# One flat list of steps for eight sequences, in another order

## The chip, the cores and the metric

The kernel runs on one NeuronCore of a Trainium2 chip. The number that counts is the time of one execution on the device in microseconds (us); of several executions the median is given. A profile is one execution recorded by the hardware: each instruction with its engine, its start and its length. The engines are TensorE (PE, matmuls; PEld is its weight load), VectorE (DVE), ScalarE (ACT), GpSimd (POOL) and SyncE (SP, which here issues nearly all DMAs). Each engine works through its own instructions in the order in which the program lists them, and waits where an operand or a buffer isn't ready.

## What is computed

Eight sequences of 512 tokens with 256 channels go through a feed-forward half step, causal attention with 16 heads, and the same feed-forward half step again; each has a layer norm ahead of it and a residual around it. A `butterfly` is ten stages of 2x2 mixing over 1024 channels. All is float32.

```python
x = x + 0.5 * ffn(layernorm(x))
x = x + attn(layernorm(x))
x = x + 0.5 * ffn(layernorm(x))

def ffn(x):      # the same weights both times
    h = butterfly(x @ W_exp + b_exp, up_weights)
    h = butterfly(gelu(h + up_bias), down_weights)
    return h @ W_con + b_con + down_bias

def attn(x):     # q, k, v: 16 heads of 32 channels
    scores = where(causal, q @ k.T / sqrt(16), -inf)
    return concat(softmax(scores) @ v) @ Wo
```

## The kernel before

**Folding.** At the start the butterflies are multiplied into the weights, so that a feed-forward is two products: up (256 to 1024, then gelu) and down (1024 to 256). While this is done, the up steps of sequence 0 and the first layer norm of sequence 1 are computed as well (lines 718 to 742). None of that is touched by the change.

**Steps.** After it, the whole work of all eight sequences is cut into steps of one to three microseconds of TensorE, and a list written out by hand in the source (`ORDER`, line 636) says in which order the steps are put into the program. Every engine's own order follows from this one list. A word of it is a letter, a number and a sequence; the letters are

- `f`, `g`: one of 8 up steps of the first and of the second feed-forward (`up_steps`, line 378): a product into a PSUM tile `ph`, then a gelu on ACT into the tile `g` (line 392). The first step of such a group allocates `g`; there is one buffer for it.
- `F`, `G`: one of 8 down half steps (`down_steps`, line 396): four of them fill one PSUM tile `py`, then DVE adds it to the residual `x` (line 414). `G` also stores `x` to DRAM (line 416).
- `s`, `a`, `x` with `1`, `a` or `2` for the three layer norms: statistics (DVE, with a power on POOL), normalization with a 32x32 transpose on DVE, and the way into the transposed tile `xnt`. Each comes in two halves. For nearly all, `x` is a pair of DMA steps: first a write to DRAM (`td`, line 365), then four reads back (`xnt`, line 372). For the attention norm of sequence 0 and the last norm of sequence 7 it is two transposes on TensorE (line 207) instead.
- `q`, `v`: one of 8 query and key steps, one of 4 value steps: a product into PSUM, then a copy by ACT (lines 437, 451).
- `u0` to `u9`: a unit of scores. TensorE writes `sc` (line 492), which is one tile of four PSUM banks for all units. DVE adds the causal mask and takes the row's minimum of the negated scores (line 506), then ACT takes the exponential (line 519). The ten units of a sequence are the entries of `UNITS`, line 465.
- `t`: DVE transposes a unit's exponentials into `pr` (line 537). `m`: DVE adds the transposed reciprocals of the row sums (line 547), then SP issues 16 DMAs that carry `pr` to the tile `pt` (line 563; one buffer). `p`: 32 matmul records of `pt` with `v` into `pa` (line 576), then a DVE product into `ot` (line 583). There are four groups of heads, so `m0` to `m3` and `p0` to `p3` for each sequence.
- `w`: one of 4 output products (`po`); two fill a PSUM tile, which DVE adds to `x` (line 602).
- `l`: the load of a later sequence's `x` (line 106).

The PSUM tiles of `f`, `g`, `F`, `G`, `q`, `v` and `w` share three buffers (`ps_a`). Exponential and gelu use different tables of ACT; a change from the one to the other shows as an `ACT_TABLE_LOAD` in the profile.

`ORDER` has one list for each sequence, and the loop at line 748 goes through them one after the other. A word's sequence is given relative to the list in which it stands: in the list of sequence 7, `w-1` is an output step of sequence 6, and `p-3` the last product of sequence 6. The lists of sequence 0 and 7 begin

```python
0: """7F+0 x1+1 sa+0 aa+0 F+0 sa+0 x1+1 2f+1 aa+0 xa+0 f+1 xa+0 f+1 s1+2 2q+0 f+1 s1+2 u0 a1+2 2q+0 u1 v
7: """q+0 u0 q+0 u1 2G-2 t0 u2 p-3 t1a w-1 t1b t2a G-2 m0 u3 w-1 G-2 s2-1 u4 v t2b v t4a t3 2w-1 t4b v
      s2-1 v p0 m1 q+0 2a2-1 q+0 u5 q+0 u6 t5 G-2 q+0 t6b u7 2x2-1 t6a G-2 t7a p1 m2 u8 2G-2 g-1 t8 2g-1
      u9 t9a 2g-1 l+1 g-1 t9b t7b p2 2g-1 2G-1 m3 3G-1 p3 2w+0 s2+0 2w+0 a2+0 s2+0 2G-1 a2+0 G-1 2x2+0 8g+0
```

Of the kernel before, what the change touches and what calls it, by code (L numbers as in the profile page):

```python
# [48 lines left out]
def macaron_kernel(  # L49
# [19 lines left out]
    B, N, C = x.shape  # L69
# [34 lines left out]
    def load_x(b):  # L104
        xt[b] = resid.tile([P, NT, C], F32, name=f"x_{b}", tag="x", bufs=4)
        nc.sync.dma_start(out=xt[b], in_=x[b].rearrange("(t p) c -> p t c", p=P))
# [358 lines left out]
    UNITS = [(0, 0), (1, 0), (2, 0), (0, 1), (1, 1), (0, 2), (1, 2), (2, 2), (0, 3), (1, 3)]  # L465
# [77 lines left out]
    def turn_sums(b, g):  # L543

        zr = lnp.tile([P, 4, NT], F32, name=f"zr_{b}_{g}", tag="zr")
        nc.vector.reciprocal(zr.rearrange("p h q -> p q h"), kept["zs", b][:, g])
        nc.vector.transpose(
            kept["pr", b, g][:, :, 4 * NSLOT :, :],
            zr.rearrange("p h (q o) -> p h q o", o=1).to_broadcast([P, 4, NT, 32]),
        )  # L550

    def move(b, g, pool):

        pr = kept.pop(("pr", b, g))
        pt = kept["pt", b, g] = pool.tile([P, 4, ROW, 32], F32, name=f"pt_{b}_{g}", tag="pt")
        ends = (b, g) == (B - 1, NG - 1)
        if ends:
            for i in range(4):
                nc.vector.tensor_copy(pt[bass.ts(i, 32), i], pr[bass.ts(i, 32), i])
        for d in range(1 if ends else 0, 4):  # L560
            for i in (0, 2, 1, 3):
                j = i ^ d
                nc.sync.dma_start(out=pt[bass.ts(j, 32), i], in_=pr[bass.ts(i, 32), j])  # L563
# [50 lines left out]
            else:  # L614
                step()

    def attention_steps(b, pool):
        def moved(g):
            turn_sums(b, g)
            move(b, g, pool)  # L620

        return {
            "u": lambda n: score_unit(b, *UNITS[n], pool),
            "t": lambda n, part=0: turn(b, *UNITS[n], part, pool),
            "m": moved,
            "p": lambda g: times_v(b, g, pool),
        }

    ORDER = {
        0: """7F+0 x1+1 sa+0 aa+0 F+0 sa+0 x1+1 2f+1 aa+0 xa+0 f+1 xa+0 f+1 s1+2 2q+0 f+1 s1+2 u0 a1+2 2q+0 u1 v
              q+0 v t0 t1b u2 v 2f+1 t1a f+1 t2a m0 a1+2 u3 t2b 2F+1 u4 x1+2 t3 2F+1 t4b sa+1 v x1+2 q+0 t4a F+1
              u5 p0 m1 t5 u6 3F+1 aa+1 sa+1 2q+0 u7 f+2 t6b aa+1 t6a f+2 xa+1 f+2 xa+1 u8 t7a p1 2f+2 m2 2f+2 t8
              f+2 q+1 t7b q+1 u9 q+1 t9a t9b 2q+1 p2 m3""",  # L640
        1: """u0 F+1 q+0 u1 2F+1 t0 u2 F+1 t1b 2q+0 t1a u3 t2a p-3 m0 u4 2w-1 s2-1 a2-1 w-1 v w-1 s2-1 v t2b a2-1
              F+1 u5 v t3 x2-1 sa+1 3F+1 t4b v x2-1 aa+1 u6 p0 2g-1 sa+1 s1+2 aa+1 t4a xa+1 m1 g-1 a1+2 t5 g-1
              s1+2 4g-1 G-1 u7 xa+1 G-1 a1+2 x1+2 t7a x1+2 4G-1 t6a t6b u8 p1 m2 u9 t8 2G-1 f+2 q+1 f+2 t7b t9b
              f+2 q+1 f+2 t9a f+2 q+1 p2 f+2 m3""",
        2: """u0 2q+0 u1 t0 q+0 2f+1 u2 2q+0 t1a u3 p-3 t2a t1b u4 m0 2w-1 F+1 t2b u5 F+1 t3 F+1 t4a w-1 t4b F+1
              l+2 s2-1 w-1 2v s2-1 v 2a2-1 v F+1 sa+1 x2-1 F+1 u6 p0 F+1 t6a x2-1 m1 F+1 t6b t5 aa+1 sa+1 aa+1
              xa+1 7g-1 u7 s1+2 g-1 G-1 u8 t7a p1 t7b xa+1 m2 a1+2 u9 2G-1 q+1 G-1 s1+2 a1+2 t8 t9b 3G-1 x1+2 G-1
              t9a q+1 x1+2 2q+1 p2 m3""",
        3: """u0 2q+0 l+2 f+1 t0 4f+1 u1 2f+1 u2 p-3 w-1 t1b w-1 s2-1 q+0 t2a t1a u3 t2b m0 v 2w-1 v u4 t3 q+0
              a2-1 v f+1 u5 s2-1 a2-1 t4b v t4a 4F+1 u6 p0 x2-1 F+1 x2-1 m1 sa+1 2F+1 s1+2 u7 F+1 sa+1 aa+1 4g-1  # L650
              t7a aa+1 t5 t6a 2g-1 t6b xa+1 u8 p1 g-1 xa+1 g-1 m2 t7b u9 q+1 s1+2 q+1 a1+2 G-1 t9a a1+2 x1+2 t8
              t9b 2G-1 q+1 x1+2 G-1 q+1 p2 m3""",
        4: """u0 3G-2 t0 q+0 u1 G-2 q+0 u2 t1b 2f+1 q+0 t1a u3 p-3 l+2 u4 w-1 t3 v w-1 f+1 t2a w-1 s2-1 m0 v w-1
              t4b s2-1 2f+1 t2b 2a2-1 q+0 f+1 v x2-1 f+1 2s1+2 f+1 2F+1 v u5 p0 u6 x2-1 F+1 t4a F+1 m1 F+1 u7 t6a
              3F+1 g-1 sa+1 t5 2g-1 aa+1 sa+1 aa+1 g-1 t7a 2g-1 t6b u8 p1 2xa+1 g-1 m2 a1+2 g-1 t8 G-1 u9 2G-1
              a1+2 q+1 t7b G-1 2x1+2 t9a 2q+1 G-1 q+1 t9b p2 m3""",
        5: """u0 3G-2 u1 q+0 t0 2q+0 u2 f+1 t1b 2f+1 t1a u3 p-3 u4 w-1 t2a v t2b w-1 s2-1 q+0 l+2 m0 f+1 s1+2 v t3
              v t4a f+1 u5 t4b a2-1 w-1 f+1 w-1 f+1 s2-1 a2-1 v x2-1 f+1 s1+2 F+1 u6 p0 x2-1 m1 t6b 2F+1 a1+2 u7
              3F+1 t5 a1+2 F+1 sa+1 F+1 g-1 t7a x1+2 sa+1 g-1 aa+1 2g-1 aa+1 u8 t6a xa+1 p1 xa+1 4g-1 m2 x1+2 u9
              t9b t8 2q+1 2G-1 q+1 G-1 t9a t7b G-1 p2 m3""",  # L660
        6: """u0 q+0 2G-2 u1 G-2 q+0 u2 G-2 t1a t1b 2f+1 t0 t2a 2f+1 u3 p-3 m0 u4 w-1 t2b w-1 v 2w-1 v s2-1 q+0 v
              t4b t4a v t3 s2-1 f+1 u5 p0 m1 2f+1 a2-1 t5 f+1 u6 q+0 a2-1 F+1 t6b q+0 F+1 u7 F+1 t6a F+1 x2-1 t7a
              p1 x2-1 t7b m2 u8 sa+1 3F+1 u9 F+1 2g-1 sa+1 aa+1 g-1 aa+1 g-1 xa+1 t9a g-1 t8 g-1 t9b p2 xa+1 2g-1
              2q+1 m3""",
        7: """q+0 u0 q+0 u1 2G-2 t0 u2 p-3 t1a w-1 t1b t2a G-2 m0 u3 w-1 G-2 s2-1 u4 v t2b v t4a t3 2w-1 t4b v
              s2-1 v p0 m1 q+0 2a2-1 q+0 u5 q+0 u6 t5 G-2 q+0 t6b u7 2x2-1 t6a G-2 t7a p1 m2 u8 2G-2 g-1 t8 2g-1
              u9 t9a 2g-1 l+1 g-1 t9b t7b p2 2g-1 2G-1 m3 3G-1 p3 2w+0 s2+0 2w+0 a2+0 s2+0 2G-1 a2+0 G-1 2x2+0 8g+0
              8G+0""",
    }
    LNS = {"a": "at", "1": "f1", "2": "f2"}  # L670
    queues = {}

    def next_of(key, b, make):
        if (key, b) not in queues:
            queues[key, b] = make()
        return queues[key, b].pop(0)

    def sequence(b, pool):
        for token in ORDER[b].split():
            times, rest = (int(token[0]), token[1:]) if token[0].isdigit() else (1, token)  # L680
            what, kind, at = rest[0], "", 0
            if what in "sax":
                kind, rest = rest[1], rest[1:]
            if what in "ut":
                part = "ab".find(rest[-1])
                n = int(rest[1]) if part >= 0 else int(rest[1:])
            elif len(rest) > 1:
                at = int(rest[1:])
            for _ in range(times):
                if what == "u":  # L690
                    attention_steps(b, pool)["u"](n)
                elif what == "t":
                    attention_steps(b, pool)["t"](n, max(part, 0))
                elif what == "m":
                    attention_steps(b, pool)["m"](at)
                elif what == "p":
                    attention_steps(b - (at < 0), pool)["p"](abs(at))
                elif what == "l":
                    if b + at < B:
                        load_x(b + at)  # L700
                elif b + at < B:
                    c, ln = b + at, LNS.get(kind)
                    make = {
                        "q": lambda: qk_steps(c),
                        "v": lambda: v_steps(c),
                        "w": lambda: wo_steps(c),
                        "f": lambda: up_steps(c, "f1"),
                        "F": lambda: down_steps(c, "f1", store=False),
                        "g": lambda: up_steps(c, "f2"),
                        "G": lambda: down_steps(c, "f2", store=True),  # L710
                        "s": lambda: [partial(ln_stats, c, ln, half) for half in range(2)],
                        "a": lambda: [partial(ln_apply, c, ln, half) for half in range(2)],
                        "x": lambda: ln_steps(c, ln),
                    }[what]
                    next_of(what + kind, c, make)()


    with fold, tc.manual_schedule():
        nc.scalar.activation(ones[:, :1], ones[:, 1:2], AF.Copy)
# [15 lines left out]
        for i in range(HIGH - 1, -1, -1):  # L735
            cur, _ = high_stage(cur, i, dnc_sb, "dn", C, NBLK // 2)
# [8 lines left out]
    ps_o = ctx.enter_context(tc.tile_pool(name="ps_o", bufs=1, space=bass.MemoryType.PSUM))  # L745
    with tc.tile_pool(name="attn", bufs=1) as attn, tc.manual_schedule():
        kept["sc"] = ps_u.tile([P, 4, 512], F32, name="sc", tag="u")
        for b in range(B):
            sequence(b, attn)


def _turned(x):
# [87 lines left out]
```

## Time and profile before

| | us |
|---|---|
| median of 3 runs | 872.11 (870.77 to 872.52) |
| the profiled execution, whole | 870.19 |
| its span, first to last instruction | 868.2 |
| TensorE busy | 847.7 |
| VectorE busy | 629.4 |
| ScalarE busy | 517.8 |
| GpSimd busy | 92.2 |
| DMA rows on SP's queue | 55.8% of 16 engines |

A row of the timeline reads: start in us from the span's start, length in us, engine, line, operation, the tiles written and read, shape, number of instructions, and in brackets how long the engine had been idle and what released it. A row of the waits reads: engine, tile and line that waited, what it waited for, then the total in us, the number of times and the longest. Ends of matmuls are modelled, so a step's length on TensorE is better read from one start to the next. fp32 matmuls appear as two records each: an `f`, `g`, `q` or `v` step is 16 records, an `F`, `G` or `w` step and a `p` step 32.

### The profile page before, as it was taken

The page shows a single profiled execution, that of the slowest core. Times are in us where ns is not written, and L with a number is a line of the kernel's source. Part 1 is how long each engine was busy: PE and PEld are TensorE (multiplying, and loading weights), DVE is VectorE, ACT ScalarE, POOL GpSimd, SP SyncE. Part 2 cuts the span into 40 slices and gives each one's busy share as a digit, 9 for nine tenths or more (in the row PEclk, how much of TensorE's full clock was granted, in tenths as well). Part 3 has the DMA queues.
Part 4 walks back from the last instruction along what each step waited for, and adds up shares of the span by engine and source line. Part 5 has one row for each costly group of instructions (what it writes and reads, how often), then busy time and mean ns, then how long its engine had stood idle before and what let it go on. Part 6 is the DMA issues. An engine that isn't in the chain of part 4 may idle for free.

```text
span 868.2 us, 28463 instructions
## 1 busy us (share of the span) xinstructions
PE 847.7 (98%) x11914; PEld 370.1 (43%) x11914; DVE 629.4 (73%) x1815; ACT 517.8 (60%) x1359; POOL 92.2 (11%) x123
## 2 busy tenths in 40 slices
PE   8999999999999999999999999999999999989898
PEld 7443524444334443443443434335344343433454
DVE  7948985997579685699777585888567794977430
ACT  6618686654585474776585654865746764747210
POOL 6511000011001010010102010021000100010010
PEclk9999999999999999999999999999999999999999
DMA  9210766637656568267765277557684577367400
GB/s 334 70 50 18 206 183 153 159 110 204 179 135 159 146 175 225 54 178 189 195 172 135 83 192 193 134 140 202 166 188 123 127 190 200 99 174 198 129 14 26
DMA packets 52832, 130.41 MB, mean 150 GB/s; under 512 B 10849, under 2 KB 32609, under 8 KB 52705
## 3 DMA queue, kind: packets, MB, share of 16 engines
q1 hardware_dynamic: 52560, 128.57, 55.8%
q8 instruction: 94, 1.54, 0.8%
q14 instruction: 34, 0.27, 0.1%
q10 hardware_dynamic: 144, 0.02, 0.0%
HBM read 21.80 MB, written 15.20 MB: 43 GB/s over the span
## 4 chain that ended last, share of the span: by engine, by line
PE 80%; SPq 5%; DVE 5%; DMA 4%; ACT 3%; issue 1%; DVEq 0%; ACTq 0%
PE ph_f L352 22%; PE py_f L352 22%; PE pp L352 11%; PE sc L492 8%; PE po L352 6%; PE pv L352 6%; SPq L563 5%; PE pa L576 5%; DVE e L506 3%; DMA out_dram<-x 1%; ACT e L519 1%; DMA pt<-pr 1%; DVE pr L537 1%; DMA wexp_sb<-in_wexp_t_dram 1%; DMA x<-in_x_dram 1%
## 5 line engine op out<-in xcount | busy, mean ns | idle before, releaser
L519 ACT ACTIVATE e<-e,nm 128x128 f32<-128x128 f32 (+3 forms) x512 | 280.4, 549 | 93.6 <-DVE nm L506 93.2
L506 DVE CUSTOM_DVE_ANT_0 e<-sc,mask 128x384 f32<-128x384 f32 (+2 forms) x384 | 196.4, 552 | 98.4 <-PE sc L492 97.8
L352 PE MATMUL py_f<-wdn_sb,g_f 128*32 128x256 f32 x4096 | 232.4, 380 | 0.0
L352 PE MATMUL ph_f<-xnt_f,wup_sb 128*32 128x512 f32 x2048 | 228.6, 593 | 0.6 <-ACT g_f L392 0.3
L537 DVE STREAM_TRANSPOSE pr<-e 128x1536 f32<-128x1536 f32 (+2 forms) x128 | 171.2, 1356 | 19.8 <-ACT e L519 19.8
L352 PEld LDWEIGHTS py_f<-wdn_sb,g_f 128*32 128x32 f32 x4096 | 131.9, 110 | 100.2 <-issue 19.3
L392 ACT ACTIVATE g_f<-ph_f,bup_sb 128x512 f32<-128x512 f32 x128 | 84.7, 686 | 90.6 <-PE ph_f L352 90.1
L352 PEld LDWEIGHTS ph_f<-xnt_f,wup_sb 128*32 128x32 f32 x2048 | 65.2, 110 | 139.7 <-issue 113.7
L519 ACT ACTIVATION_READ_ACCUMULATOR e<-e,nm 128x1 f32 x512 | 96.0, 188 | 0.0
L492 PE MATMUL sc<-kt,qt 32*64 32x512 f32 (+5 forms) x2048 | 86.6, 431 | 6.9 <-DVE nm L506 4.9
L576 PE MATMUL pa<-pt,v 128*32 128x512 f32 (+3 forms) x1024 | 75.4, 435 | 5.3 <-DMA pt<-pr 3.5
L169 POOL TENSOR_TENSOR rstd_f<-mv_f,mhalf 128x2 f32<-128x2 f32 x32 | 22.4, 702 | 481.6 <-DVE mv_f L167 463.2
L492 PEld LDWEIGHTS sc<-kt,qt 32*64 32x64 f32 x2048 | 40.8, 130 | 61.2 <-issue 27.3
L352 PE MATMUL pp<-xnt_at,wq_sb 128*32 128x512 f32 x512 | 61.0, 594 | 0.0
L352 PE MATMUL pp<-xnt_at,wk_sb 128*32 128x512 f32 x512 | 61.0, 593 | 0.0
L352 PE MATMUL po<-wo_sb,ot 128*32 128x256 f32 x1024 | 59.7, 380 | 0.4 <-DVE ot L583 0.4
L352 PE MATMUL pv<-wv_sb,xnt_at 128*32 128x512 f32 x512 | 59.7, 593 | 0.0
L576 PEld LDWEIGHTS pa<-pt,v 128*32 128x32 f32 x1024 | 31.8, 109 | 60.6 <-issue 50.1
L414 DVE SCALAR_TENSOR_TENSOR x<-py_f,x 128x512 f32<-128x512 f32 (+1 forms) x34 | 22.1, 649 | 44.4 <-PE py_f L352 44.4
L200 POOL TENSOR_TENSOR x<-x,bhalf 128x512 f32<-128x512 f32 x32 | 41.0, 1283 | 120.4 <-DVE xn_f L183 117.4
L519 ACT ACT_TABLE_LOAD x28 | 35.9, 1283 | 23.9 <-DVE nm L506 23.7
L583 DVE TENSOR_TENSOR ot<-pa,pt 128x512 f32<-128x512 f32 x32 | 21.8, 680 | 35.8 <-PE pa L576 35.8
(89 smaller groups left out, 577.3 us busy)
## 6 DMA issues: line engine op xcount, KB each, us to landing
pt<-pr SPq DMA_DIRECT2D x508, 176.0 KB, 4.3
td_f<-tx_f SPq DMA_DIRECT2D x14, 512.0 KB, 4.5
xnt_f<-td_f SPq DMA_DIRECT2D x56, 128.0 KB, 2.9
x<-in_x_dram SPq DMA_DIRECT2D x8, 512.0 KB, 6.1
td_at<-tx_at SPq DMA_DIRECT2D x7, 512.0 KB, 2.6
xnt_at<-td_at SPq DMA_DIRECT2D x28, 128.0 KB, 3.0
out_dram<-x SPq DMA_DIRECT2D x14, 256.0 KB, 4.2
wexp_sb<-in_wexp_t_dram SPq DMA_DIRECT2D x2, 514.0 KB, 7.7
```

Of the source, the lines that this page charges most:

```text
L169: nc.gpsimd.tensor_tensor(rstd, mv[:, :, 1], mhalf, ALU.pow)
L200: nc.gpsimd.tensor_tensor(x2, x2, bhalf.rearrange("p (o c) -> p o c", o=1).to_broadcast([P, 2, C]), ALU.add)
L352: nc.tensor.matmul(out[c : c + 32], lhsT=lhsT[:, c : c + 32], rhs=rhs, start=start, stop=stop)
L392: nc.scalar.activation(g[:, fc, :], ph[:, :N], AF.Gelu, bias=bup_sb[:, fc : fc + 1])
L414: nc.vector.scalar_tensor_tensor(mine, py[:, i + 1 - n : i + 1, :], 0.5, mine, ALU.mult, ALU.add)
L492: nc.tensor.matmul(sc[s : s + ROWS, j, at + low : at + high], lhsT=kept["q", b, gg][r, bass.ds(qb * P + s, ROWS)], rhs=kept["k", b, gg][r, ...
L506: nc.vector.tensor_tensor_reduce(out=e[:, j, at : at + n], in0=sc[:, j, at : at + n], in1=mask[:, N - n :] if qb else mask_first, scale=-1 ...
L519: nc.scalar.activation(e[:, j, at : at + n], e[:, j, at : at + n], AF.Exp, scale=-1.0, bias=nm[:, qb, gg, j : j + 1], accum_out=zs[:, gg, ...
L537: nc.vector.transpose(pr[:, :, :, qb : qb + 3 * n - 2 : 3, :].rearrange("p j h k r -> p h k j r"), blocks[:, :, :n])
L563: nc.sync.dma_start(out=pt[bass.ts(j, 32), i], in_=pr[bass.ts(i, 32), j])
L576: nc.tensor.matmul(by_row[r, :, kb * 32 :], lhsT=v[:, kb, bass.ds(g * P + j * HD, HD)], rhs=pt[:, :, bass.ds(j * NSLOT + SLOT[kb] + kb, NT ...
L583: nc.vector.tensor_tensor(kept["ot", b][:, g, :].rearrange("p (i q r) -> p i q r", i=4, r=32), pa.rearrange("p (i q r) -> p i q r", i=4, r ...
```

## The change

The eight relative lists become one flat list, `STEPS`, in which each word carries its absolute sequence after an `@`, and a small reader (`perform`) takes the place of `sequence` and `attention_steps`. The multiset of the 786 steps is the same; every step issues the instructions it issued before. What differs is the order, and it differs all along: steps of one sequence may now stand anywhere among those of another (`u0@1` ahead of `t9b@0`, for example). The diff, cut:

```diff
-    ORDER = {
-        0: """7F+0 x1+1 sa+0 aa+0 F+0 sa+0 x1+1 2f+1 aa+0 xa+0 f+1 xa+0 f+1 s1+2 2q+0 f+1 s1+2 u0 a1+2 2q+0 u1 v
...
-    }
+    STEPS = """
+        2x1@1 s1@2 2F@0 a1@2 s1@2 F@0 a1@2 F@0 sa@0 f@1 4F@0 sa@0 2f@1 2aa@0 2xa@0 f@1 2q@0 f@1 u0@0 2q@0 u1@0
+        v@0 t0a@0 t1b@0 q@0 2x1@2 v@0 u2@0 v@0 f@1 t1a@0 f@1 t2a@0 m0@0 u3@0 f@1 v@0 F@1 t2b@0 u4@0 F@1 t3a@0
...
+        F@7 sa@7 3g@5 2aa@7 xa@7 g@5 t8a@6 g@5 xa@7 t9a@6 t9b@6 p2@6 2g@5 t7b@6 q@7 m3@6 q@7 g@5 u0@7 2q@7 u1@7
+        t0a@7 2G@5 u2@7 t1b@7 p3@6 t1a@7 G@5 t2a@7 m0@7 G@5 t2b@7 2w@6 u3@7 2w@6 u4@7 t3a@7 v@7 s2@6 v@7 s2@6
+        q@7 v@7 t4a@7 t4b@7 a2@6 v@7 p0@7 m1@7 a2@6 2x2@6 q@7 u5@7 u6@7 2q@7 t5a@7 t6a@7 u7@7 t6b@7 t7a@7 2G@5
+        p1@7 m2@7 u8@7 2G@5 g@6 t8a@7 g@6 t7b@7 g@6 u9@7 t9b@7 3g@6 t9a@7 p2@7 2g@6 3G@6 m3@7 3G@6 p3@7 2w@7
+        s2@7 2w@7 s2@7 2a2@7 2G@6 2x2@7 8g@7 8G@7
+    """
...
+    def perform(token, pool):
+        times, rest = (int(token[0]), token[1:]) if token[0].isdigit() else (1, token)
+        rest, c = rest.split("@")
+        what, c = rest[0], int(c)
+        for _ in range(times):
+            if what == "u":
+                score_unit(c, *UNITS[int(rest[1])], pool)
+            elif what == "t":
+                turn(c, *UNITS[int(rest[1])], "ab".find(rest[2]), pool)
+            elif what == "m":
+                turn_sums(c, int(rest[1]))
+                move(c, int(rest[1]), pool)
+            elif what == "p":
+                times_v(c, int(rest[1]), pool)
+            elif what == "l":
+                load_x(c)
...
-        for b in range(B):
-            sequence(b, attn)
+        for token in STEPS.split():
+            perform(token, attn)
```

More of the change, by code (lines that the diff above doesn't have):

```diff
@@ L615, in run @@
                 step()
[L617 to L626, printed above, removed]
-        }
-    ORDER = {
-        0: """7F+0 x1+1 sa+0 aa+0 F+0 sa+0 x1+1 2f+1 aa+0 xa+0 f+1 xa+0 f+1 s1+2 2q+0 f+1 s1+2 u0 a1+2 2q+0 u1 v
[L638 to L669, printed above, removed]
@@ new lines, in macaron_kernel @@
+    STEPS = """
+        2x1@1 s1@2 2F@0 a1@2 s1@2 F@0 a1@2 F@0 sa@0 f@1 4F@0 sa@0 2f@1 2aa@0 2xa@0 f@1 2q@0 f@1 u0@0 2q@0 u1@0
+        v@0 t0a@0 t1b@0 q@0 2x1@2 v@0 u2@0 v@0 f@1 t1a@0 f@1 t2a@0 m0@0 u3@0 f@1 v@0 F@1 t2b@0 u4@0 F@1 t3a@0
+        2F@1 q@0 sa@1 F@1 t4b@0 t4a@0 u5@0 p0@0 m1@0 q@0 t5a@0 F@1 u6@0 aa@1 2F@1 sa@1 q@0 u7@0 f@2 aa@1 xa@1
+        t6b@0 t6a@0 2f@2 u8@0 p1@0 xa@1 3f@2 t7a@0 m2@0 q@1 t8a@0 q@1 u9@0 q@1 t7b@0 t9a@0 2q@1 u0@1 t9b@0 2f@2
+        p2@0 m3@0 u1@1 F@2 t0a@1 t1a@1 2F@2 u2@1 2F@2 q@1 u3@1 2q@1 sa@2 t1b@1 t2a@1 p3@0 m0@1 u4@1 2w@0 v@1
+        t3a@1 s2@0 w@0 a2@0 w@0 s2@0 a2@0 v@1 u5@1 v@1 2F@2 v@1 t4b@1 2x2@0 t4a@1 u6@1 F@2 s1@3 p0@1 t2b@1 t6b@1
+        m1@1 a1@3 4g@0 aa@2 s1@3 t6a@1 4g@0 sa@2 t5a@1 u7@1 a1@3 x1@3 t7a@1 2G@0 aa@2 G@0 xa@2 x1@3 u8@1 xa@2
+        G@0 p1@1 m2@1 u9@1 4G@0 q@2 t7b@1 q@2 f@3 t9a@1 f@3 u0@2 t8a@1 f@3 t9b@1 2f@3 p2@1 m3@1 q@2 f@3 t0a@2
+        q@2 u1@2 t1b@2 3q@2 u2@2 2f@3 q@2 t2a@2 p3@1 w@1 t1a@2 u3@2 F@3 m0@2 w@1 u4@2 t4a@2 w@1 v@2 s2@1 w@1
+        s2@1 l@4 F@3 2a2@1 t3a@2 3v@2 u5@2 s1@4 F@3 x2@1 t2b@2 x2@1 t4b@2 p0@2 m1@2 F@3 sa@3 F@3 u6@2 3F@3 t6a@2
+        t6b@2 3g@1 s1@4 sa@3 2aa@3 a1@4 2xa@3 3g@1 t5a@2 u7@2 t7a@2 2g@1 p1@2 m2@2 u8@2 t8a@2 4G@1 2q@3 t7b@2
+        q@3 a1@4 u9@2 t9a@2 G@1 x1@4 q@3 p2@2 q@3 2G@1 x1@4 t9b@2 m3@2 G@1 u0@3 3f@4 u1@3 3f@4 p3@2 u2@3 2w@2
+        s2@2 f@4 l@5 t2b@3 t1b@3 t1a@3 t0a@3 t2a@3 v@3 f@4 2q@3 u3@3 v@3 m0@3 v@3 q@3 t3a@3 u4@3 2w@2 s2@2 v@3
+        2a2@2 x2@2 u5@3 x2@2 3F@4 u6@3 t4b@3 F@4 p0@3 F@4 t4a@3 F@4 m1@3 u7@3 F@4 t6a@3 F@4 2sa@4 2aa@4 3g@2
+        t7a@3 s1@5 2g@2 xa@4 t5a@3 g@2 u8@3 t6b@3 g@2 t7b@3 g@2 p1@3 xa@4 m2@3 u9@3 t9b@3 G@2 2q@4 a1@5 s1@5
+        a1@5 G@2 x1@5 t8a@3 t9a@3 u0@4 3G@2 q@4 x1@5 G@2 p2@3 m3@3 u1@4 2G@2 t1a@4 t0a@4 4q@4 t1b@4 u2@4 q@4
+        2f@5 u3@4 p3@3 v@4 t2a@4 u4@4 2w@3 t4b@4 v@4 l@6 m0@4 w@3 s2@3 t2b@4 a2@3 2f@5 s1@6 f@5 w@3 s2@3 2v@4
+        t3a@4 a2@3 x2@3 t4a@4 x2@3 a1@6 f@5 u5@4 2f@5 p0@4 m1@4 u6@4 s1@6 a1@6 2F@5 x1@6 F@5 u7@4 3F@5 sa@5 aa@5
+        F@5 t6b@4 F@5 t7a@4 sa@5 aa@5 xa@5 2g@3 t6a@4 xa@5 2g@3 p1@4 t5a@4 m2@4 2g@3 u8@4 2g@3 u9@4 t9b@4 t7b@4
+        t9a@4 G@3 x1@6 G@3 t8a@4 2q@5 2G@3 u0@5 G@3 p2@4 G@3 q@5 m3@4 u1@5 G@3 2q@5 u2@5 G@3 t0a@5 f@6 t1a@5
+        2q@5 t2a@5 l@7 t1b@5 u3@5 f@6 p3@4 m0@5 t2b@5 f@6 u4@5 q@5 s1@7 a1@7 4w@4 u5@5 v@5 s2@4 a2@4 s1@7 t4a@5
+        3v@5 t3a@5 3f@6 s2@4 a1@7 f@6 u6@5 f@6 F@6 t4b@5 x1@7 a2@4 t6a@5 p0@5 u7@5 x1@7 2x2@4 F@6 m1@5 t5a@5
+        2F@6 u8@5 F@6 t6b@5 2F@6 sa@6 F@6 g@4 sa@6 3g@4 2aa@6 xa@6 u9@5 t7a@5 g@4 xa@6 p1@5 m2@5 3g@4 G@4 t9a@5
+        t8a@5 3q@6 t7b@5 u0@6 t0a@6 G@4 q@6 G@4 t9b@5 p2@5 m3@5 u1@6 5G@4 f@7 u2@6 t1a@6 2f@7 t1b@6 f@7 t2b@6
+        p3@5 t2a@6 m0@6 w@5 v@6 w@5 u3@6 w@5 s2@5 w@5 s2@5 t3a@6 2q@6 u4@6 t4a@6 3v@6 u5@6 p0@6 t4b@6 m1@6 t5a@6
+        a2@5 4f@7 u6@6 a2@5 2q@6 F@7 t6b@6 x2@5 F@7 t6a@6 x2@5 u7@6 t7a@6 F@7 p1@6 m2@6 u8@6 3F@7 u9@6 F@7 sa@7
+        F@7 sa@7 3g@5 2aa@7 xa@7 g@5 t8a@6 g@5 xa@7 t9a@6 t9b@6 p2@6 2g@5 t7b@6 q@7 m3@6 q@7 g@5 u0@7 2q@7 u1@7
[3 more added lines that the diff above has]
+        s2@7 2w@7 s2@7 2a2@7 2G@6 2x2@7 8g@7 8G@7
@@ L676, in next_of @@
         return queues[key, b].pop(0)
[L678 to L715, printed above, removed]
@@ new lines, in perform @@
+    def perform(token, pool):
[14 more added lines that the diff above has]
+                load_x(c)
+            else:
+                ln = LNS[rest[1]] if what in "sax" else None
+                make = {
+                    "q": lambda: qk_steps(c),
+                    "v": lambda: v_steps(c),
+                    "w": lambda: wo_steps(c),
+                    "f": lambda: up_steps(c, "f1"),
+                    "F": lambda: down_steps(c, "f1", store=False),
+                    "g": lambda: up_steps(c, "f2"),
+                    "G": lambda: down_steps(c, "f2", store=True),
+                    "s": lambda: [partial(ln_stats, c, ln, half) for half in range(2)],
+                    "a": lambda: [partial(ln_apply, c, ln, half) for half in range(2)],
+                    "x": lambda: ln_steps(c, ln),
+                }[what]
+                next_of(rest, c, make)()
```

## The prediction

> **What bounds the kernel.** The page comes first: its span and the share of each engine.
>
> ```profile
> span 868.2 us, 28463 instructions
> ...
> PE 847.7 (98%) x11914; PEld 370.1 (43%) x11914; DVE 629.4 (73%) x1815; ACT 517.8 (60%) x1359; POOL 92.2 (11%) x123
> ```
>
> TensorE is busy for 98% of the span. The same instructions in another order can't shorten that, so only time in which TensorE stands still can be won, and every new wait of it is lost. Second, what TensorE waited for (total, times, longest):
>
> ```profile
> PE sc L492 <- DVE nm L506: 4.9, 10, 0.8
> PE pa L576 <- DMA pt<-pr: 3.5, 2, 2.0
> ...
> PE pa L576 <- DMA out_dram<-x: 1.5, 1, 1.5
> ```
>
> These lengths hide the modelled ends of matmuls, so I read waits from start to start in the timeline. A `q`, `f`, `g` or `v` step takes 1.72 us (768.01 to 769.73 below), an `F`, `G` or `w` step 1.73, a `p` 2.15, a `u` about 1.0, and a change from another step to `u` costs 0.11 more. Wherever two starts lie further apart than these, TensorE waited. Summed over the trace that comes to some 18 us after the folding; 2 us of it are differences under 0.03 us, which any order keeps. The common case, in the timeline of TensorE:
>
> ```profile
> 309.17 1.11 PE L492 MATMUL sc<-kt,qt 32*64 32x512 f32 x16
> 310.21 2.36 PE L576 MATMUL pa<-pt,v 128*32 128x512 f32 x32
> 312.98 1.02 PE L492 MATMUL sc<-kt,qt 32*64 32x320 f32 x32 [0.41 <-DVE nm L506]
> ```
>
> A `p` alone stands between two units. The second waits until DVE has read `sc`: 2.77 us from `pa` to `sc` where 2.15 + 0.11 would do, so 0.50 lost.
>
> **What the new order takes away.** (1) `u p u` with nothing else for TensorE occurs nine times in the old list (after `u3` in sequences 1, 2, 4, 5 and 6, after `u5` in 0 and 4, after `u8` in 1 and 2), in the new one never: 9 x 0.50 = 4.5 us. (2) In sequence 7, `u0 q u1` becomes `u0 2q u1`: `sc` began 2.77 after the `q` at 733.51 where 1.83 would do, 0.94. (3) A `w` right after `p3` of sequence 6 had to wait for `ot`; two `G` and other work now stand between: 0.60. (4) The products at 141.09 and 160.26 started 0.21 and 0.33 late behind their DMAs; the new list gives them 1.2 and 0.5 us of further cover. (5) `p0` of sequence 7 started at 765.86, 3.44 after the `v` ahead of it, so 1.72 late. From the end of `u2` at 741.87 it took 24.0 us to get there (masks, exponentials, transposes, 16 DMAs). The new list has 23.4 us of TensorE work in that place, against 21.6: about 0.3 remains, 1.4 are won. Together 4.5 + 0.94 + 0.60 + 0.54 + 1.4 = 8.0 us.
>
> **What it adds: the first `f` of sequence 1.** The old list has all eight `F` of sequence 0 ahead of it, the new one four. The timelines of TensorE and of SP, and the DMA issues of that window (number, size of each, median us from issue to landing):
>
> ```profile
> 37.87 14.02 PE L352 MATMUL py_f<-wdn_sb,g_f 128*32 128x256 f32 x256
> 51.71 0.61 PE L352 MATMUL ph_f<-xnt_f,wup_sb 128*32 128x512 f32 x4
> ```
>
> ```profile
> 43.22 0.34 SPq L365 DMA_DIRECT2D td_f<-tx_f  x1
> 45.89 1.75 SPq L372 DMA_DIRECT2D xnt_f<-td_f  x4
> ```
>
> ```profile
> xnt_f<-td_f SPq DMA_DIRECT2D x4, 128.0 KB, 3.0
> ```
>
> Eight steps took 13.84 us, 1.73 each. Four end at 37.87 + 6.92 = 44.8. What `f` reads comes from the norm of sequence 1, computed in the part that isn't changed: written at 43.22, read back from 45.89, the last of four reads issued about 47.2, 3.0 to land, so 50.3. SP has nothing ahead of these DMAs in either order, so they can't come sooner. TensorE stands still from 44.8 to 50.3: 5.5 us. Behind the waiting `f` in TensorE's order are the four other `F`, which are ready; they, the sums on DVE and everything after them start 5.5 later. The early statistics of sequence 2 (`s1`, `a1`, 6 us of DVE) fall into this hole and cost nothing.
>
> **The clock after that hole.** The longest wait in the old loop is the 2.2 us ahead of `p2` of sequence 7 at 805.28; the steps behind it have their usual length, so such a gap costs nothing further: the lower bound, 0. The upper bound is the start of the kernel, where TensorE comes from long idleness and repeats one small matmul (windows, number of matmuls in brackets):
>
> ```profile
> 2.00:4.00 2.00, 2.00 (x11) 1.00 0.78 233
> ...
> 5.00:6.00 1.00, 1.00 (x7) 1.00 0.98 365
> 6.00:7.00 1.00, 1.00 (x11) 1.00 1.09 381
> 7.00:8.00 1.00, 1.00 (x12) 1.00 1.09 353
> ```
>
> Some 6 per us until about 6.0, then 11 to 12: from 1.68 it ran 4.3 us at half speed and lost 2.2. A gap of 5.5 us lies between the two; I take the middle, 1.1.
>
> [...]
>
> **ScalarE.** Counted through both lists, exponential and gelu change places 56 times before and 66 after: 10 more loads of 1.283 us, 12.8 us on an engine that stands idle for 350. It costs something only where three steps want the three `ps_a` buffers while ACT is still at the exponentials and two loads. The old order pays 0.53 of that once (`f` of sequence 2 at 127.76). In the new one that place stays, and I count six more (a `w` of sequence 1 and an `f` of 3 behind three `q` of 2, an `f` of 2 behind four `q` of 1, a `w` of 5 behind four `f` of 7, a `g` of 4 behind three others, a `v` of 7), not all as tight: 0 to 0.53 each, a quarter of it taken, 0.8 (0 to 3.2).
>
> [...]
>
> **The end, from `p0` of sequence 7.** TensorE before:
>
> ```profile
> 765.86 2.36 PE L576 MATMUL pa<-pt,v 128*32 128x512 f32 x32 [1.54 <-DMA out_dram<-x]
> ...
> 772.36 1.12 PE L492 MATMUL sc<-kt,qt 32*64 32x512 f32 x16 [0.71 <-ACT kt L437]
> ...
> 776.17 1.02 PE L492 MATMUL sc<-kt,qt 32*64 32x320 f32 x32 [0.84 <-DVE nm L506]
> ...
> 782.53 0.69 PE L492 MATMUL sc<-kt,qt 32*64 32x256 f32 x16 [1.14 <-ACT kt L437]
> ...
> 784.91 2.34 PE L576 MATMUL pa<-pt,v 128*32 128x512 f32 x32
> ```
>
> The new list has `u5` and `u6` with nothing between. DVE, counted from the start of `p0`, still has the transposes and statistics queued before it, ends `m1` at about 5.0, a half of `a2` at 6.5 and the masks of `u5` at 9.0; `u6` starts there instead of 5.8, 3.3 late. But `p1` can't start before the DMAs of `m1`: 5.0 + 10.7 of issue + 4.3 of landing = 20.0. Before, it started at 19.05 with one `q` more in between, so the stretch loses 20.0 - (19.05 - 1.72) = 2.7, the wait of `u6` among it. `p1` to `p2` took 20.37 with 2.2 of waiting; with `m2` at 24.2 and 14.8 for its DMAs it is 19.0: 1.4 won. `p2` to `p3` stays at 15.9, but with a `G` in place of the 1.7 of waiting: 1.7 won. After `p3` only two `G` cover the last norm instead of three: 0.5 lost. Sum +0.1, uncertain by 1.5 each way.
>
> **Sum.** -8.0 + 5.5 + 1.1 + 0.8 + 0.1 = -0.5 us. The profiled execution took 870.19 with a span of 868.2; the median, 872.11, is 1.9 above it. Changes are taken to it: 872.1 - 0.5 = 871.6 us.
>
> **Rivals.** *No wait at the first `f`* (faster). `g` has one buffer, and the four late `F` still read the old one. If that keeps the whole step back and not only its gelu, the hole and the clock are gone: 871.6 - 6.6 = 865.0. Against it: only the gelu writes `g`, and TensorE's order in the trace follows the list step by step. *ACT holds the buffers* (slower). If the ten further loads fall where TensorE wants a `ps_a` buffer back, all six places cost the 0.53 of the row, 3.2 in place of 0.8: 874.0. It decides where the first of three gelus starts later than the end of the third product. For it are the row at 127.76 and the loads; against it, ACT's 60%, and that three other spots of the old list with the same count of work cost nothing. *All bounds at once* (slower): this, the clock at 2.2 and the end 1.5 worse, 876.6. *Fewer waits* (faster): no loss of clock, no buffer waits, the end 1 better: 868.7.
>
> **Chances.** What can be told from no change here is about 0.2%, 1.7 us. My forecast 0.40; ACT's buffers 0.20; all bounds 0.12; no wait at `f` 0.15; fewer waits 0.13. So faster 0.30 (both fast cases and the lower edge of the forecast's), the same 0.38, slower 0.32. The forecast's own range is 869.5 to 873.5. Between the case at 865.0 and that at 876.6, with one in ten left out on each side, the range is 866.5 to 876.5.
>
> **What would show it.** A gap of some 5.5 us on TensorE ahead of the first `ph_f` after four `py_f` steps, at 44.8; steps longer than 1.72 behind it if the clock fell; no 2.77 from a `pa` to an `sc`; 67 table loads or so; `sc` of `u6` in sequence 7 some 3 us late and `p3` without a wait. I'm wrong if the gap is missing, or if new waits of 1 us and more turn up in sequences 1 to 6.

## The result, and the profile after

| | before | after |
|---|---|---|
| median, us | 872.16 (870.77 to 872.52) | 876.48 (875.65 to 877.14) |
| the profiled execution, whole | 870.19 | 875.65 |
| its span | 868.2 | 873.8 |
| TensorE busy | 847.7 | 852.6 |

The new order is slower: the ratio is 1.0059, with an interval of 1.0046 to 1.0072. That is 4.3 us in the medians and 5.5 between the two profiled executions. I had forecast no change (-0.5) and gave a slower kernel 0.32. The page of the new kernel, its span and engines, and its two groups of table loads:

```profile
span 873.8 us, 28484 instructions
...
PE 852.6 (98%) x11914; PEld 371.7 (43%) x11914; DVE 631.8 (72%) x1815; ACT 531.5 (61%) x1369; POOL 92.2 (11%) x123
...
L519 ACT ACT_TABLE_LOAD x33 | 42.3, 1283 | 22.9 <-DVE nm L506 22.5
L392 ACT ACT_TABLE_LOAD x34 | 43.6, 1283 | 15.7 <-PE ph_f L352 15.2
```

The matmuls are the same 11,914, yet TensorE is "busy" for 4.9 us more. A matmul that takes longer, or whose modelled end is stretched over a wait, counts as busy, so the busy time hides part of the loss. What TensorE waited for in the new kernel (total, times, longest):

```profile
PE ph_f L352 <- DMA xnt_f<-td_f: 5.5, 1, 5.5
PE sc L492 <- DVE nm L506: 2.7, 1, 2.7
...
PE sc L492 <- ACT kt L437: 1.3, 2, 0.7
PE pa L576 <- DMA pt<-pr: 1.1, 1, 1.1
PE po L352 <- ACT g_f L392: 1.0, 1, 1.0
PE pa L576 <- DMA out_dram<-x: 0.9, 1, 0.9
```

The ten waits of `sc` for DVE have become one. In their place stands one wait of 5.5 for the norm's DMAs, and ACT and the `pt` DMAs now hold TensorE back in places where they did not before. From one start to the next, as in the prediction, the loop from 37.6 us to the end is 5.9 longer (the folding ended 0.2 sooner). Step by step:

| | forecast | measured |
|---|---|---|
| waits that went | -8.0 | -7.8 |
| the gap at the first `f` of sequence 1 | +5.5 | +5.7 |
| slow clock behind it | +1.1 | +2.3 |
| new waits up to `p0` of sequence 7 | +0.8 | +5.0 |
| from `p0` of sequence 7 on | +0.1 | +0.8 |
| sum | -0.5 | +6.0 |

The -7.8 are eight `u p u` at 0.50 and one at 0.17, 0.94 for `u1` and 1.6 for `p0` of sequence 7, 0.60 and 0.23 at two `w`, and 0.2 at two products.

The gap, in the timeline of TensorE:

```profile
37.64 7.11 PE L352 MATMUL py_f<-wdn_sb,g_f 128*32 128x256 f32 x128
50.23 3.64 PE L352 MATMUL ph_f<-xnt_f,wup_sb 128*32 128x512 f32 x16 [5.48 <-DMA xnt_f<-td_f]
53.61 7.74 PE L352 MATMUL py_f<-wdn_sb,g_f 128*32 128x256 f32 x128
```

Four `F` from 37.64 are done at 44.55; the `f` starts at 50.23, 5.66 later (forecast: 50.3, 5.5). It then takes 3.38 to the next start in place of 1.72, and the four `F` from 53.61 take 7.56 to the start at 61.17 in place of 6.91: 2.31 more. The clock, in windows of the same kernel (window, time, TensorE busy, granted clock, DMA share, GB/s):

```profile
47.00:48.00 1.00, 0.00 (x0) 1.00 0.85 256
48.00:49.00 1.00, 0.00 (x0) 0.54 0.83 221
49.00:50.00 1.00, 0.00 (x0) 0.50 0.05 8
...
54.00:55.00 1.00, 1.00 (x16) 0.54 0.96 251
55.00:56.00 1.00, 1.00 (x25) 1.00 0.55 105
```

It falls to half at 48.08, some 3.5 after TensorE stopped, and is whole again only at 54.92. Matmuls between 50.23 and 54.92 ran at half speed, which loses half of 4.69, 2.3.

The new waits, up to `p0` of sequence 7:

| at | step | late by | it waited for |
|---|---|---|---|
| 665.52 | `w` of 5 | 1.20 | a `ps_a` buffer: three gelus behind the exponentials of `u2` |
| 334.90 | `p2` of 2 | 1.04 | its own 16 DMAs |
| 429.89 | `u0` of 4 | 0.65 | a copy into `kt` behind the exponentials of `u9` |
| 496.25, 99.30, 600.50 | `F` | 0.41, 0.19, 0.16 | a gelu whose output it reads, behind exponentials and a load |
| 146.16, 257.38, 529.68, 768.96 | `f`, `f`, `q`, `v` | 0.35, 0.35, 0.28, 0.23 | a buffer, behind exponentials |
| 391.14 | `u6` of 3 | 0.17 | `sc`, which DVE reads only after two halves of a norm |

The costliest of them in the timeline, on ACT, DVE and TensorE:

```profile
659.42 0.51 ACT L519 ACTIVATE e<-e,nm 128x256 f32<-128x256 f32 x1
...
663.48 1.28 ACT L392 ACT_TABLE_LOAD   x1
...
664.66 0.65 DVE L583 TENSOR_TENSOR ot<-pa,pt 128x512 f32<-128x512 f32 x1
664.78 1.84 ACT L392 ACTIVATE g_f<-ph_f,bup_sb 128x512 f32<-128x512 f32 x3
...
665.52 1.93 PE L352 MATMUL po<-wo_sb,ot 128*32 128x256 f32 x32 [1.02 <-ACT g_f L392]
```

Eight exponentials run from 659.42 to 663.37, a load until 664.76, and only then come three gelus, which hold all three buffers. The first is done at about 665.4, and the `w` starts. `ot`, which the `w` reads, is ready at 665.31, nearly as late; which of the two counts can't be read from this trace.

### The profile page after: what moved, and what is told of

Same layout as the page of the kernel before. It is cut to its first block, busy times and chain, and to the rows that moved or that the text cites. A ratio compares the mean times of both kernels' runs of the same rounds, so it can differ in the third digit from the quotient of the medians.

```text
span 873.8 us, 28484 instructions
## 1 busy us (share of the span) xinstructions
PE 852.6 (98%) x11914; PEld 371.7 (43%) x11914; DVE 631.8 (72%) x1815; ACT 531.5 (61%) x1369; POOL 92.2 (11%) x123
## 4 chain that ended last, share of the span: by engine, by line
PE 73%; DVE 9%; ACT 8%; DMA 3%; SPq 2%; issue 1%; POOL 0%; DVEq 0%; ACTq 0%; POOLq 0%
PE py_f L352 21%; PE ph_f L352 19%; PE pp L352 10%; PE sc L492 7%; PE pa L576 7%; PE po L352 6%; ACT e L519 5%; PE pv L352 4%; SPq L563 2%; DVE e L506 2%; DVE pr L537 1%; DMA pt<-pr 1%; ACT L519 1%; DVE high_dn L253 1%; DVE xn_f L183 1%
## 5 line engine op out<-in xcount | busy, mean ns | idle before, releaser
L352 PEld LDWEIGHTS py_f<-wdn_sb,g_f 128*32 128x32 f32 x4096 | 131.7, 110 | 100.9 <-issue 18.9
L392 ACT ACT_TABLE_LOAD x34 | 43.6, 1283 | 15.7 <-PE ph_f L352 15.2
```

The costliest lines, as they stand in the source:

```text
L352: nc.tensor.matmul(out[c : c + 32], lhsT=lhsT[:, c : c + 32], rhs=rhs, start=start, stop=stop)
L392: nc.scalar.activation(g[:, fc, :], ph[:, :N], AF.Gelu, bias=bup_sb[:, fc : fc + 1])
```

## The experiments

The gap and the clock first. My theory after the result: the gap and the clock account for 8.0 us of the loss, and small waits on ACT and the DMAs for the rest. Rivals: the gap's end would be paid for elsewhere, or the slow steps had nothing to do with the gap.

**The first `f` behind eight `F`.**

```diff
-2F@0 a1@2 s1@2 F@0 a1@2 F@0 sa@0 f@1 4F@0 sa@0 2f@1
+2F@0 a1@2 s1@2 F@0 a1@2 F@0 sa@0 4F@0 f@1 sa@0 2f@1
```

> The changed kernel with one step moved: the first f of sequence 1 goes behind all eight F of sequence 0 (51.5 us) in place of behind four. Theory (hole and slow clock): TensorE's gap of 5.66 ahead of that f disappears and so do the 2.31 that the 16 matmuls of f and the F behind it ran too long (1.67 + 0.65): 876.5 - 8.0 = 868.5, with every step up to 60 us at its usual length. Rival (the norm's DMAs are late whatever stands ahead, or the four F pushed forward displace work that then waits elsewhere): the gap shrinks, but the other half turns up at the transposes of sequence 0's norm or in the first units; 871 to 874. Rival (only the gap goes, the slow steps have another cause than the gap): 870.8.

Measured: 869.26, where the old kernel had 870.75 beside it; ratio 0.9975 (0.9963 to 0.9987). With the 1.0059 of the changed kernel, 0.84% or 7.3 us are won by this one move, of the 8.0 expected. In its trace the gap and every slow step up to 60 us are gone. What is missing lies, in the profiled execution (869.91), at waits that hang on DMAs and at the end: `p2` of sequence 2 waits 1.66 in place of 1.04 and `p2` of sequence 7 1.78 in place of 1.24, but a second execution of the changed kernel has 1.52 and 1.69 there, so this need not come from the edit; and `p0` to `p1` of sequence 7 takes 20.61 in place of 19.65, with the clock halved for 6.83 us of it.

**The same gap in the old order.** The other way round: the `f` goes behind four `F` there.

```diff
-7F+0 x1+1 sa+0 aa+0 F+0 sa+0 x1+1 2f+1 aa+0 xa+0
+2x1+1 4F+0 f+1 3F+0 sa+0 aa+0 F+0 sa+0 f+1 aa+0 xa+0
```

> The old kernel with the first f of sequence 1 behind four F in place of eight, and both halves of the norm's DMAs listed ahead of it; nothing else. Theory: the gap of 5.66 and the 2.31 of slow clock appear here too and nothing takes them back: 872.1 + 8.0 = 880.1, with the waits from 100 us on as in the old kernel. Rival (later slack absorbs part of it): 874 to 878, with the waits of the old kernel at 102 to 160 us smaller.

Measured: 879.84 against 870.75, ratio 1.0108 (1.0093 to 1.0123), 9.1 us. The gap is 5.64, the slow clock 1.30. Another 1.7 comes from the edit: only one `f` is left between the last `F` and the transposes of sequence 0's norm, and the second of these waits. `p3` of 0 and `p2` of 5 are 0.6 and 0.7 later than in the old kernel. Little of the gap is absorbed later: the waits that get shorter (the most at `p0` of sequence 7, 1.26 in place of 1.70) win less than those two lose.

**Shorter and longer gaps.** The `f` behind six, five and three `F`, and two of the kernels a second time.

> The changed kernel with the first f of sequence 1 behind six F. The gap ahead of it should be 50.23 - (37.64 + 6 x 1.727) = 2.23 us. If the clock is a matter of how long TensorE stood, this gap is like the 2.20 ahead of p2 of sequence 7 in the old kernel and costs nothing further: f and F behind it at 1.72 and 1.73, time 876.5 - 8.0 + 2.2 = 870.7. Rival (any wait at this place slows the clock, for instance because what follows a burst of DMA reads is slow): again 2.3 lost behind it, 873.0.

> The changed kernel with the first f of sequence 1 behind five F: a gap of 50.23 - (37.64 + 5 x 1.727) = 3.96 us. Between the gap that cost nothing (2.20) and the one that cost 2.31 (5.66). If the loss of clock is a threshold below 3.96, 2.3 are lost again and the time is 868.5 + 3.96 + 2.3 = 874.8; if the threshold lies above, 872.5; if the loss grows with the gap, something between, such as 1.2.

> The kernel with the first f of sequence 1 behind five F, once more. A gap of 3.93 us; no loss in its first profile. [...] Rival (a threshold between 3.93 and 5.66): never a fall. Only a fall would tell.

> The changed kernel with the first f of sequence 1 behind three F: a gap of 50.23 - (37.64 + 3 x 1.727) = 7.41 us. [...] Rival (the loss grows with the time TensorE stood): more than 2.31, 3 or over. Time 876.5 + 1.7 less the difference in the clock's loss, 876.5 to 878.5.

> The changed kernel once more, for the clock alone. In its first profile the granted clock fell to 0.50 at about 48.3, 3.5 us after TensorE stopped, and came back at about 54.8; in the old kernel with the same gap it fell at 49.4, 4.7 us after, and came back at 52.8: 2.31 and 1.30 lost. [...] Rival (the loss belongs to the place and the gap): 2.31 again within 0.1, falling at 48.3.

| `f` behind | gap | clock falls, is whole again | lost | time of this execution |
|---|---|---|---|---|
| 6 `F` | 2.18 | no | 0 | 870.73 |
| 5 `F` | 3.93 | no | 0 | 872.15 |
| 5 `F`, again | 3.91 | 49.51, 52.93 | 1.42 | 873.40 |
| 4 `F`, old order | 5.64 | 49.43, 52.85 | 1.30 | 879.34 |
| 4 `F`, changed kernel | 5.66 | 48.08, 54.92 | 2.31 | 875.65 |
| the same, again | 5.70 | 48.92, 55.75 | 2.76 | 876.77 |
| 3 `F` | 7.37 | 46.94, 53.77 | 1.77 | 877.36 |

The fall and the return are worked out from the granted clock of the windows in which it changes. Two executions of one kernel, five `F`, the first without a fall and the second with one:

```profile
49.00:50.00 1.00, 0.00 (x0) 1.00 0.06 8
50.00:51.00 1.00, 0.78 (x8) 1.00 0.77 315
...
52.00:53.00 1.00, 1.00 (x24) 1.00 0.00 0
```

```profile
49.00:50.00 1.00, 0.00 (x0) 0.76 0.00 0
50.00:51.00 1.00, 0.95 (x8) 0.50 0.90 369
...
52.00:53.00 1.00, 1.00 (x8) 0.54 0.00 1
```

The same `f` after the same gap took 1.72 us to the next start there (50.22 to 51.94) and 3.14 here (50.05 to 53.19). So neither the place nor the length of the gap alone decides; a threshold between 3.93 and 5.66, my rival for the second run, falls. Nor does the loss grow with the gap, my rival for three `F`: 7.37 lost 1.77, less than the 2.31 of 5.66; its time, 877.36, lay within the 876.5 to 878.5 that I had put down. The second run of the changed kernel lost 2.76, so its rival, 2.31 again within 0.1, falls as well. The clock stays low for 3.42 or for 6.83, which is 3.42 or twice that, in all five falls of this table.

The clock fell behind a shorter wait, too. In the changed kernel it falls a second time at 781.95, 0.84 after `u6` of sequence 7 had started behind its wait of 2.76, and is whole again at 785.36. In a later experiment (`u6` behind a `q`) it falls at 778.21, behind waits of 1.24 and 1.64. The 3.41 us ahead of the one and of the other:

```profile
778.54:781.95 3.41, 0.84 (x32) 1.00 0.83 230
```

```profile
774.80:778.21 3.41, 1.36 (x36) 1.00 1.02 243
```

TensorE was busy (by its modelled ends) for 25% and 40% of these. In the first execution with five `F` it stood idle for 3.75 us on end, and the granted clock stayed at 1.00. What decides on a fall these runs don't show.

Nor do they show why the clock is whole again after 3.42 us or only after twice that. In the 3.42 behind the fall TensorE was busy for 78% (the old order with four `F`) and 84% (five `F` again) in the two executions in which it was whole at their end, and for 37% and 63% in the two runs of the changed kernel, which had it at 0.50 for another 3.42.

**The middle waits.** Three moves by one step, with the first `f` behind eight `F`:

```diff
-q@3 p2@2 q@3 2G@1
+q@3 G@1 p2@2 q@3 G@1
...
-t8a@3 t9a@3 u0@4 3G@2 q@4
+t8a@3 t9a@3 G@2 u0@4 2G@2 q@4
...
-p3@5 t2a@6 m0@6 w@5 v@6 w@5 u3@6
+p3@5 t2a@6 m0@6 v@6 w@5 w@5 u3@6
```

> The changed kernel with the first f of sequence 1 behind eight F, and three moves by one step: a G ahead of p2 of sequence 2, a G ahead of u0 of sequence 4, and a v between p3 of sequence 5 and the w behind it. Before these, TensorE waited 1.66, 0.65 and 1.20 at the three places. First two: both gone, -2.3 together (p2 is late behind its DMAs, u0 behind a copy that stands after a unit's exponentials; a step of 1.73 covers either). Third, theory (three gelus stand behind the exponentials of u2 and a table load, and hold all three ps_a buffers): the v needs the same buffer and waits 1.1 in place of the w. Rival (the w waits for the DVE product into ot behind p3): v goes at once and hides it, the wait is 0. Time 867.0 by the theory, 865.8 by the rival, where the old kernel has 870.8.

Measured: 866.24 in one execution, where the old kernel has 870.72, 0.8 below what I expected. `p2` and `u0` go without a wait. At the third place, ACT and TensorE:

```profile
655.09 1.84 ACT L392 ACTIVATE g_f<-ph_f,bup_sb 128x512 f32<-128x512 f32 x3
...
655.83 1.92 PE L352 MATMUL pv<-wv_sb,xnt_at 128*32 128x512 f32 x16 [1.01 <-ACT g_f L392]
```

The `v` doesn't read `ot`, yet it starts 1.20 late as the `w` did, again 0.74 after the first gelu began. The buffers hold it, and the rival falls. Then the other way, `u2` one `f` later in place of the third move:

```diff
-f@7 u2@6 t1a@6 2f@7 t1b@6 f@7 t2b@6 p3@5
+2f@7 u2@6 t1a@6 f@7 t1b@6 f@7 t2b@6 p3@5
```

> As the kernel with the v, but at the third place p3, w and v stand as in the changed kernel and u2 of sequence 6 goes one f later, so that one gelu fewer stands behind its exponentials. Theory (gelus hold the buffers): a free buffer is there for the w; what is left is the wait for ot, that is ot's end less the end of p3, about 1.0 (DVE takes 0.65 for ot, and started it 0.4 after p3's last matmul). So 1.20 becomes 1.0 at most and the two causes stand one behind the other. Rival (gelus alone): 0. Rival (ot alone): 1.20 as before.

```profile
656.20 0.65 DVE L583 TENSOR_TENSOR ot<-pa,pt 128x512 f32<-128x512 f32 x1
...
656.90 0.64 PE L352 MATMUL po<-wo_sb,ot 128*32 128x256 f32 x8 [0.85 <-DVE ot L583]
```

Measured: 866.66 in one execution. One buffer is free, part of the `w` runs, and the rest waits for `ot`, 1.05 in all. So the two causes stand one behind the other, and taking one away wins 0.15 of 1.20.

**`u5` next to `u6` in sequence 7.** To the kernel before this one:

```diff
-q@7 u5@7 u6@7 2q@7 t5a@7
+q@7 u5@7 q@7 u6@7 q@7 t5a@7
```

> The kernel before this one with one of the two q behind u6 of sequence 7 put between u5 and u6. Theory: u6's wait falls from 2.76 to 0.9 and the q's 1.6 goes, but p1 can't start before the DMAs of m1, 19.6 behind p0, so of the 2.8 won some 2 turn up as a wait ahead of p1 or of what stands before it: p0 to p1 stays at 19.5 to 20.6 and the time changes by less than 1. Rival (u5 next to u6 costs its 2.8): p0 to p1 falls to 17.5 and the time by 2.8. Whole kernel, against the old one at 870.8: 866.5 by the theory, 864.5 by the rival.

TensorE with `u5` next to `u6` (the kernel with the `v`; in the one that was edited `u6` waits as long), and after this edit:

```profile
771.37 1.02 PE L492 MATMUL sc<-kt,qt 32*64 32x320 f32 x32 [2.69 <-DVE nm L506]
```

```profile
771.18 1.02 PE L492 MATMUL sc<-kt,qt 32*64 32x320 f32 x32 [0.84 <-DVE nm L506]
...
775.20 0.69 PE L492 MATMUL sc<-kt,qt 32*64 32x256 f32 x16 [1.15 <-DVE nm L506]
777.54 0.69 PE L492 MATMUL sc<-kt,qt 32*64 32x256 f32 x16 [1.64 <-ACT kt L437]
778.16 5.35 PE L352 MATMUL py_f<-wdn_sb,g_f 128*32 128x256 f32 x64
783.32 2.33 PE L576 MATMUL pa<-pt,v 128*32 128x512 f32 x32
```

Measured: 867.19 (866.51 to 867.34), a ratio of 0.9955 (0.9940 to 0.9970) to the old kernel; the kernel without the edit had 866.66 in one execution. `u6` waits 0.93 in place of 2.76, but it starts 8.58 after `p0` as it did before. Behind it `u7` waits 1.24 for DVE and its second half 1.64 for the copy into `kt`, which stands on ACT behind the exponentials of `u6`; and with the clock halved from 778.21 to 781.63 two `G` take 5.16 in place of 3.46. `p0` to `p1` is 20.72, before 20.30. So the time hardly changed, as I expected, but not for my reason: the last of the DMAs of `m1` was issued at 776.9, none of those whose landing the trace shows took more than 4.6, and `p1` started at 783.32 without a wait.

**Only the nine `u p u`.** In the old kernel, at each of the nine places, one step from close by goes in between the two units, ahead of the `p` or behind it, such as

```diff
-u3 p-3 u4 w-1 t2a v t2b
+u3 v p-3 u4 w-1 t2a t2b
...
-u5 p0 u6 x2-1 F+1 t4a
+u5 p0 F+1 u6 x2-1 t4a
```

> The old kernel with the nine places u p u broken up: at each, one step from a few places away (F, G, v or q) stands between p and u. Theory: 8 x 0.50 and 0.17 of waits disappear and nothing else changes, 4.2 won: 870.8 - 4.2 = 866.6. Rival (the step that was moved is missing where it stood, as cover for a p or a buffer there): half of it or less is won, 868.5 to 871.

Measured: 868.73 (867.60 to 870.36) against 870.72, ratio 0.9976 (0.9966 to 0.9987), 2.0 us. The nine waits are gone, all 4.2 us, and about half came back. Two of the places in TensorE's timeline:

```profile
224.91 2.35 PE L352 MATMUL ph_f<-xnt_f,wup_sb 128*32 128x512 f32 x20 [0.57 <-DVE x L414]
```

```profile
449.74 1.49 PE L352 MATMUL pv<-wv_sb,xnt_at 128*32 128x512 f32 x12 [0.40 <-ACT g_f L392]
```

Behind one of the two `G` that were brought forward, an `f` now waits 0.75 for the buffer that the `G` group holds until DVE has added it; two of the three `v` that were brought forward wait 0.47 each for a buffer behind gelus; a `q` of sequence 7 waits 0.34, by its row for the DMAs of its norm. That is 2.0, and the rival is right: a step that fills a gap brings, at three of the nine places, its own demand on a buffer.

**All cures together**: eight `F` ahead of the `f`, `G` ahead of `p2` and `u0`, `u2` later and the `v` ahead of the `w`.

> The changed kernel with all cures at once: the first f of sequence 1 behind eight F, a G ahead of p2 of sequence 2 and of u0 of sequence 4, and at p3 of sequence 5 both u2 of sequence 6 one f later and a v ahead of the w. Theory (the w's wait of 1.20 had two causes, one behind the other): with a buffer free the v goes at once and covers the wait for ot; nothing is left there. 866.2 - 1.2 = 865.0 where the old kernel has 870.7, a ratio of 0.9935. Rival (the u2 that comes later, or other steps, pay for it elsewhere, as in the old kernel with its nine places broken up, where half was given back): 866 to 867.

Measured: 865.83 (865.37 to 866.58) against 870.48, ratio 0.9937 (0.9918 to 0.9955). It is faster than both kernels, by 0.6% and 1.2%. At the third place the `v` starts at once, but it takes the free buffer, and the `w` behind it waits 0.75 for the next gelu: 0.45 of 1.20 is won there, not all.

## Why the prediction was wrong

*What the order takes away* was right: -8.0 forecast, -7.8 measured, with `p0` of sequence 7 at 1.6 in place of 1.4. At 160.26 I had counted 0.33 as won; `p3` of sequence 0 is still 0.35 late.

*The gap* was right in place, cause and size: 5.66 for 5.5, and 7.3 us come back when one step is moved behind the four `F`.

*The clock* did fall behind the gap, but the term was too small: 2.31 in the profile where I took the middle between 0 and 2.2. The runs show that no single row could give it: with a gap of 5.6 to 5.7 the loss was 1.30, 2.31 and 2.76, two of the three above my upper bound. The row that I took for the lower bound, 2.2 of waiting, is one wait at a granted clock of 1.00; that others like it cost nothing further didn't follow from it, and behind the 2.76 ahead of `u6` in the new order the clock did fall, which the prediction lacks.

*ScalarE* is the step that failed. I wrote "0 to 0.53 each, a quarter of it taken, 0.8 (0 to 3.2)". What the term was to hold, the new waits in the loop, came to 5.0. Three things went wrong in it. Of the six places that I named, four cost something (`w` of 5, `f` of 3, `f` of 2, `v` of 7): 2.13 together, well over the 0.8. One of them, the `w`, cost 1.20, over twice the 0.53 that I had as the ceiling of one place: there three gelus stood behind 4.0 us of exponentials and a load, in the row at 127.76 behind 2.9 us and a load. And I looked only for a lack of buffers. The same late ACT holds back an `F` that reads the gelu's output and a `u0` that reads a copy; that is another 1.4. The answer of the trace on `g` between 490 and 500 us shows it:

```profile
who waited for it (us, times):
  PEld py_f L352: 1.0, 2
```

The tables themselves were counted rightly (67 loads), but most of the waiting is behind exponentials, and a load makes it longer by its 1.28.

A term was missing altogether: products that come too early for their DMAs in the middle of the list. DVE ended `m2` of sequence 2 at 319.66, and `p2` had its turn at 333.86, 14.2 us later. My own least figure from an `m` to its `p` was 14.8, and I had not held the middle of the new list against it, only the end. By my own sign, new waits of 1 us and more in sequences 1 to 6, I was wrong at two places, this one and the `w`. In the new kernel's timeline:

```profile
319.73 10.48 SPq L563 DMA_DIRECT2D pt<-pr  x16
...
334.90 2.36 PE L576 MATMUL pa<-pt,v 128*32 128x512 f32 x32 [0.86 <-DMA out_dram<-x]
```

The issues end at 330.2, and the product starts 4.7 later, 15.2 after `m2`. (The row names a store of `x`, but that was issued at 330.32 and landed 5.2 later, when the product had begun.) One `G` ahead of it took the wait away.

*The end* was right in most of its parts: `u6` 2.76 late (forecast 3.3), `p1` to `p2` 19.41 (19.0), `p2` to `p3` 15.94 (15.9). `p0` to `p1`, 19.65 (20.0), was right by luck. The DMAs of `m1`, which were to set it, were issued by 786.8 and took at most 4.6, so they had landed 18.9 after `p0`, and `p1` waited for nothing. The time behind `u6` went into the second fall of the clock, which made a `q` 1.62 longer, and into a wait of 0.37 of `u7` for the copy into `kt`; with five `F`, in the execution without that fall, this wait is 1.89 and `p0` to `p1` 19.52. So the exponentials of `u6` ahead of that copy set the time, and the fall cost less than 0.2. And the last norm had too little cover: about 1.1 lost, not 0.5.

My rival with *all bounds at once*, 876.6, had the right sign and came within 0.1 us of the time, but by other terms: its clock was right, its worse end was not, and it had neither the `F` nor the product of sequence 2. I gave it 0.12 because I let each term take its mean; the clock's came out above its upper bound, and ACT's, with 2.13 at the places that I named, in the upper half of its own.

## What to carry to other kernels

Where TensorE is busy for 98% of the span, a list that is put in another order must be gone through for every wait that it can make, not only for those that it takes away: for each product the work between it and its last DMA issue, for each step the buffer it needs, and for each reader the engine that writes for it. A gap can cost more than its length, by the matmuls behind it that run at a granted clock of 0.50: with 2.2 it cost only itself here, with 3.9 once 1.42 more and once not, with 5.6 and over more in all four runs, 1.3 to 2.8. Where another wait stands behind the slow steps, as at `u7` in the changed kernel, the fall can cost next to nothing (under 0.2). And a wait that is taken away is won only if the step that fills it finds its buffer and its input: of nine waits worth 4.2 us, 2.0 were won.

## What was not expected of the hardware

The granted clock came back 3.42 us after its fall, or 6.83, in the five falls at the first `f`. Towards the end of the list it was 3.41 in the changed kernel, 3.42 with `u6` behind a `q` and 6.83 with the first `f` behind eight `F`. It fell behind a wait of 2.76 in the changed kernel, yet not behind 3.93 in the first execution with five `F`. And the same kernel, with the same gap of 3.9 us, lost 0 in one execution and 1.42 in the next, so a single execution can't price such a gap.
